# Latent layer: TensorE's transposes of the probabilities are issued behind a step's scores and exponentials, where they were issued in front of them

## The chip, the cores and the metric

The kernel runs on one core of one Trainium2 chip. The metric is the device time of one execution in microseconds (us). The kernel before took 2329.43 us, the median of three runs (2329.16, 2329.43 and 2336.82 us). The profile comes from one more execution, which took 2339.59 us. A core has five engines that matter here: TensorE (PE in the profile, with its weight loads as PEld), VectorE (DVE), ScalarE (ACT), GpSimd (POOL) and SyncE (SP). SyncE does no arithmetic; in this kernel it issues the transfers. Each engine works through its own instructions in the order in which the program issued them, and waits where one of them needs a result or a buffer that isn't there yet.

## The reference

The input is two sequences of 1024 tokens with 128 features. Four attention layers (called a, b, c and d here), each followed by a feed-forward part, are added to it in turn:

```
x = x + attn_a(ln(x));  x = x + ffn(ln(x))     # a: shared keys and values, no mask
x = x + attn_b(ln(x));  x = x + ffn(ln(x))     # b: causal
x = x + attn_c(ln(x));  x = x + moe(ln(x))     # c: causal, "latent"
x = x + attn_d(ln(x));  x = x + moe(ln(x))     # d: causal, with biases
```

All have 16 heads of 64. The change concerns layer c:

```
q      = x @ Wq                       # 16 heads of 64
latent = x @ Wkv_down                 # 32 numbers for each token
k, v   = latent @ Wk_up, latent @ Wv_up
attn   = softmax(where(causal, q @ k.T / 8, min))
out    = (attn @ v) @ Wout
```

The kernel multiplies Wq with Wk_up, and Wv_up with Wout, once at the start. From there on, layer c's keys and values are both the latent itself, and its products contract over, or yield, 32 rows of the array where the other layers have 64.

## The kernel before

**Units and steps.** The work of a layer is cut into units: one sequence and one pair of heads, so 16 units a layer. The queries are 8 tiles of 128. A causal unit has five steps, by their query tiles: [7], [6, 0], [5, 1], [4, 2] and [3]. Tile n sees n + 1 tiles of keys, so the two-tile steps have 8 tiles of keys, and [3] has 4. One loop runs over the steps of all units; its body writes out the order of the work by hand, and the order of each engine's instructions is exactly that of the program (`manual_schedule`).

**What a step does.** Let s be the step that is new. `scores` (L634 for the products, L649 for layer c's masks) multiplies queries with keys on TensorE, into two PSUM buffers `sc`, one for each head h of the pair; in layer c the products of both heads are issued in turns, and the masks of both follow. VectorE finds each row's maximum (L678, `nmax`), and `exponentials` (L689) has ScalarE write exp(score - max) into an SBUF tile `pr`, of which there are two buffers. A step's scores can't start on a head before the exponentials of the step ahead have read that head's `sc`. One step later, `normalize` divides: a reciprocal on VectorE (L697), and four (or two) multiplications on GpSimd (L701). Two steps later (`st` is step s - 2) the probabilities are transposed so that they can be multiplied with the values.

**Two ways to transpose.** The queries are grouped in four blocks of 256 (qb, two tiles each). Blocks 2 and 3 (tiles 4 to 7) of a causal layer are "blocked": VectorE transposes 32 x 32 pieces of `pr` into `slots` (L771), and when both tiles of a block are there, `blocks_moved` has SyncE issue 16 transfers from `slots` to `prT` (L746). Blocks 0 and 1 (tiles 0 to 3) go through TensorE: 128 x 128 transposes into a PSUM tile `pp` (L788), for two tiles of keys at most and both heads, and a copy by ScalarE into `prT` or `prT_four` (L789). Tile 0 takes 2 transposes and 1 copy, tile 1 takes 4 and 1, tile 2 takes 6 and 2, and tile 3 takes 8 and 2. `pp` is one of the uses of a pool of three PSUM buffers, in turn with the projections, the output products and the feed-forward part.

**Where they stand.** Because `st` is two steps back, tile 0 is transposed when [4, 2] is new, tile 1 when [3] is, and tiles 2 and 3 when the next unit's [7] and [6, 0] are; when [5, 1] is new there is only VectorE's part. In the loop body, `transposes(st)` comes first. Then come GpSimd's additions to x (`add_products`, L889), perhaps an early piece of the feed-forward part (`side_part`), then `scores` and `exponentials` of s, then `out_product` (L866 and a copy, L873), a piece of the next unit's projection (L532, L540), pieces of the feed-forward part, and the products with the values for blocks that were completed earlier (`weigh`, L836 and L840 in layer c, and a copy of their sum, L856). Which blocks may be weighed is kept in `late`: a block gets its `ready` step when both of its tiles are transposed, at once for blocks 0 and 1 and two steps on for the blocked ones, whose transfers take time. The products with the values of block 3 so stand in the [7] and [6, 0] of the next unit, those of blocks 0 and 1 in its [5, 1], and those of block 2 in its [4, 2].

Of the kernel before, what the change touches and what calls it, by code (L numbers as in the profile page):

```python
# [27 lines left out]
TPA = AB // P  # L28
# [8 lines left out]
def kernel(ctx: ExitStack, tc: tile.TileContext, a: dict, out: bass.AP):  # L37
# [223 lines left out]
    def moe_group(nm, b, g, last, xT, eng=nc.gpsimd, other=None):  # L261
# [139 lines left out]
    layers = [  # L401
        dict(nm="a", causal=False, kind="shared", ffn=dense_group, fnm="f"),
        dict(nm="b", causal=True, kind="full", ffn=dense_group, fnm="g"),
        dict(nm="c", causal=True, kind="latent", ffn=moe_group, fnm="m"),
        dict(nm="d", causal=True, kind="bias", ffn=moe_group, fnm="n"),
    ]
# [37 lines left out]
    def xT_tile(li, b):  # L444
        return lnp.tile([P, S], F32, tag="xT", name=f"xT_{li}{b}", bufs=2)
# [129 lines left out]
    def tag_of(u):  # L575
        li, b, p = u
        return f"{layers[li]['nm']}{b * NPAIR + p}"
# [20 lines left out]
    def blocked(u, qb):  # L598

        if qb not in BLOCKED[layers[u[0]]["kind"]]:  # L600
            return 0
        nk = keys(u, qb * TPA + TPA - 1)
        return nk if layers[u[0]]["causal"] else nk - 1

    def keys(u, qt):
        return qt + 1 if layers[u[0]]["causal"] else NT
# [99 lines left out]
    def prT_of(u, qb):  # L706


        nk = keys(u, qb * TPA + TPA - 1)
        odd = nk == NT and qb % 2 and not layers[u[0]]["causal"]  # L710
        for part in ("second", "rest") if odd else (HOMES[nk],):
            old, held[part] = held.get(part), (u, qb)
            while old:
                if any(x[:2] == old for x in products):
                    weigh_some(4)
                elif any(x["key"] == old for x in late):
                    release()
                else:
                    break
        if odd:  # L720
            return prT_many[1]
        return {
            8: prT_many[0], 6: prT_many[1][:, : 12 * AB], 4: prT_four, 2: prT_many[1][:, 12 * AB :]
        }[nk]

    def blocks_of(u, qb):

        return slots[:, 1 - qb % 2, : 2 * blocked(u, qb) * AB]  # L730
# [23 lines left out]
                copies.append((o, x))  # L754
        probT[u, qb] = t.rearrange("p (i t h c) -> p t h i c", t=TPA, h=2, i=4)

    def transposes(st):

        u, pr = st["u"], st["pr"]
        for qt in st["qts"]:
            qb, cols = qt // TPA, slice(qt % TPA * P, (qt % TPA + 1) * P)
            nk, nb = keys(u, qt), blocked(u, qb)
            for h in range(2 if nb else 0):
                n = min(nk, nb)
                dst = blocks_of(u, qb).rearrange(
                    "p (r t h k q) -> p t h k r q", r=4, t=TPA, h=2, q=32
                )[:, qt % TPA, h, :n]
                src = pr[:, h, st["at"][qt] : st["at"][qt] + n * P]  # L770
                nc.vector.transpose(  # L771
                    dst,
                    src.rearrange("p (k r q) -> p k r q", r=4, q=32),
                )
                yield
            if nb < nk and nb:
                o = rest_of(u, qb)[:, qt % TPA].unsqueeze(2)
            elif nb < nk:
                if (u, qb) not in probT:
                    probT[u, qb] = prT_of(u, qb).rearrange("p (h k q) -> p h k q", h=2, q=AB)  # L780
                o = probT[u, qb][:, :, :, cols]
            for k0 in range(nb, nk, 2):
                k1 = min(k0 + 2, nk)
                pt = ps_m.tile([P, 2, 2, P], F32, tag="pm", name=f"pp_{tag_of(u)}_{qt}_{k0}")
                for h in range(2):
                    for kt in range(k0, k1):
                        c0 = st["at"][qt] + kt * P
                        nc.tensor.transpose(pt[:, h, kt - k0, :], pr[:, h, c0 : c0 + P], ident)  # L788
                nc.scalar.copy(o[:, :, k0 - nb : k1 - nb], pt[:, :, : k1 - k0, :])  # L789
                yield  # L790
            complete[u, qb] = complete.get((u, qb), 0) + 1
            if nb and complete[u, qb] == TPA:
                blocks_moved(u, qb)

    def rest_of(u, qb):

        held["four"] = u, qb
        return prT_four.rearrange("p (n t h q) -> p n t h q", t=TPA, h=2, q=P)[:, qb]
# [131 lines left out]
    def drain(gen):  # L930
        for _ in gen:
            pass

    def some(queue, n):

        while n >= 1 and queue:
            try:
                next(queue[0])
                n -= 1
            except StopIteration:  # L940
                queue.popleft()
        return n
# [3 lines left out]
    def side_part():  # L946


        while side:
            try:  # L950
                said[0] = next(side[0])
                return
            except StopIteration:
                side.popleft()
        said[0] = None

    side, products, outs, waiting, complete, done = deque(), deque(), deque(), deque(), {}, {}
    adds, postponed, copies = deque(), deque(), deque()
    late = deque()
# [16 lines left out]
    def weigh_some(n):  # L976
# [7 lines left out]
        if any(x[-1] for x in [*products][:2]):  # L984
            while not part[-1]:
                part = products.popleft()
                weigh(*part)

    ctx.enter_context(tc.manual_schedule())
    drain(start_batch(0, 0, xT_tile(0, 0)))  # L990
    drain(project(units[0]))
# [93 lines left out]
    for step, (n, u, qts, i, total) in enumerate([*steps, *[(None, None, None, 0, 1)] * 4]):  # L1085
        new = None
        if n is not None:
            if n != last:
                last = n
                some(coming, 9)  # L1090
                if n + 1 < len(units):
                    nu = units[n + 1]
                    if nu[:2] != u[:2]:
                        if nu[0] == 2 and 2 not in weights:
                            wq = wpool.tile([D, H * DH], F32, tag="wq", name="wq_c")
                            nc.sync.dma_start(out=wq, in_=c_wqk.rearrange("d p h c -> d (p h c)"))
                            weights[2] = {"wq": wq}
                        elif nu[0] not in weights:
                            weights[nu[0]] = load_attn(w_names[nu[0]])
                        while nu[:2] not in xTs:  # L1100
                            side_part()
                    coming.append(project(nu))


                    if layers[nu[0]]["kind"] == "shared":
                        when = [0, 0, 1, 0, 1, 0, 0, 0]
                    elif layers[nu[0]]["kind"] == "latent":
                        when = [1, 0, 1, 0, 0]
                    elif total == NT:
                        when = [0, 1, 1, 0, 1, 1, 1, 1]  # L1110
                    else:
                        when = [1, 1, 2, 0, 2]
            new = step_of(u, qts)


        st = waiting.popleft() if len(waiting) == 2 or not new and waiting else None
        if st:
            if st["u"] not in begun:
                begun.add(st["u"])
                begin(st["u"])  # L1120
            for _ in transposes(st):
                if last_step:
                    normalize(last_step.pop())
            for qb in {qt // TPA for qt in st["qts"]}:
                if complete[st["u"], qb] == TPA:
                    x = next(x for x in late if x["key"] == (st["u"], qb))
                    x["ready"] = step + (2 if blocked(st["u"], qb) else 0)
        if last_step:
            normalize(last_step.pop())
        add_products()  # L1130
        if new and said[0] == "early":
            side_part()
            share -= 1
        if new:
            sc, nmaxs = scores(new)
            for h in range(2):
                exponentials(new, h, sc[h], nmaxs[h])
            last_step.append(new)
            waiting.append(new)
        while copies:  # L1140
            nc.scalar.copy(*copies.popleft())
        while outs:
            out_product(*outs.popleft())

        values = new and i >= (total - 2 if total == NT else total - 1)
        if new and coming and not values:
            some(coming, when[i])
        share = min(share + (1.8 if n is None else SIDE[u[0]]), 3.0)
        while share >= 1 and side:
            side_part()  # L1150
            share -= 1
            if said[0]:
                break


        while late and late[0]["ready"] is not None and late[0]["ready"] <= step:
            release()
        weigh_some(4)
        if values and coming:
            some(coming, when[i])  # L1160
# [68 lines left out]
```

## Time and profile before

| what | value |
|---|---|
| median of three runs | 2329.43 us |
| the profiled execution | 2339.59 us |
| its span, first to last instruction | 2337.9 us |
| mean granted TensorE clock | 0.954 |
| TensorE busy | 2133.6 us, 91% |
| VectorE busy | 1718.8 us, 74% |
| ScalarE busy | 1450.8 us, 62% |
| GpSimd busy | 1282.9 us, 55% |

The page gives the busy time of each engine, the span in 40 slices, the chain of work that ended last, and the costliest groups of instructions. Other views of the same trace answer for a part of the span: sums by stretch, the waits (who waited for whom), a group's instructions, and the instructions in order of time. The ends of matmuls are modelled, so a busy TensorE isn't one at its peak. "PEclk" is the clock that TensorE was granted, as a share of full speed. "<-" ahead of a name tells what ended an idle time; "issue" is idle time that nothing in the profile explains.

### The profile page before, as it was taken

Reading aid. Unit: us, or ns where it says so; the run is one execution under the profiler, and the core shown is the slowest. Engines: PE = TensorE matmul, PEld = TensorE weight load, DVE = VectorE, ACT = ScalarE, POOL = GpSimd, SP = SyncE. Lnnn points to the kernel's source line nnn. Section 1 sums busy time; section 2 is a strip of 40 time slices with the busy share of each in tenths; the row PEclk is TensorE's granted clock in tenths of the full one; section 3 lists DMA queues with packets and bytes.
Section 4 is the critical chain, followed back from the end, with each engine's and each line's share of the span. In section 5 each row is a group of like instructions: output and inputs, shape, how many; then the busy total and the mean of one; then the engine's idle time right before and its main releaser. Section 6 shows DMA issues by size and latency. Waiting matters only on the chain.

```text
span 2337.9 us, 43430 instructions
## 1 busy us (share of the span) xinstructions
PE 2133.6 (91%) x14833; PEld 1246.6 (53%) x14833; DVE 1718.8 (74%) x2695; ACT 1450.8 (62%) x3276; POOL 1282.9 (55%) x1723
## 2 busy tenths in 40 slices
PE   6999999999999999999998888888889999999986
PEld 2454444444445666666654454444456666656653
DVE  6979988999986876678668767766666656766544
ACT  3667676666765666666655566565666557665542
POOL 3767666767765554455545545545554446544441
PEclk8999999999999999999998788799899999999997
DMA  5667676666776666666654455544566456655450
GB/s 133 160 152 167 161 171 151 147 149 161 167 195 151 148 155 161 163 154 154 161 119 118 110 127 132 128 115 103 148 159 146 107 123 158 158 119 142 109 135 9
DMA packets 147195, 328.84 MB, mean 141 GB/s; under 512 B 48800, under 2 KB 59296, under 8 KB 146976
## 3 DMA queue, kind: packets, MB, share of 16 engines
q1 hardware_dynamic: 146976, 326.06, 59.0%
q8 instruction: 120, 1.97, 0.4%
q14 instruction: 99, 0.81, 0.1%
HBM read 10.27 MB, written 2.10 MB: 5 GB/s over the span
## 4 chain that ended last, share of the span: by engine, by line
PE 50%; SPq 16%; DVE 13%; ACT 8%; DMA 7%; issue 4%; POOL 2%; ACTq 0%; DVEq 0%; POOLq 0%
SPq L746 15%; PE av_a L845 6%; PE sc_a L634 6%; DMA prT<-slots 5%; PE av_d L845 5%; DVE slots L771 4%; PE sc_d L634 4%; PE sc_b L634 3%; PE av_b L845 3%; ACT pr_c L689 3%; PE sc_c L634 2%; DVE nmax_a L678 2%; DVE nmax_d L678 2%; ACT pr_b L689 2%; PE pp_d L788 2%
## 5 line engine op out<-in xcount | busy, mean ns | idle before, releaser
L689 ACT ACTIVATE pr_a<-sc_a,nmax_a 128x1024 f32<-128x1024 f32 x256 | 282.9, 1109 | 216.7 <-DVE nmax_a L678 212.8
L701 POOL TENSOR_SCALAR pr_a<-pr_a,rec_a 128x1024 f32<-128x1024 f32 x256 | 283.4, 1118 | 189.7 <-DVE rec_a L697 189.3
L701 POOL TENSOR_SCALAR pr_d<-pr_d,rec_d 128x1024 f32<-128x1024 f32 (+7 forms) x256 | 186.3, 745 | 271.0 <-DVE rec_d L697 270.7
L678 DVE TENSOR_REDUCE nmax_a<-sc_a 128x1 f32<-128x1024 f32 x256 | 298.7, 1205 | 36.1 <-PE sc_a L634 35.6
L701 POOL TENSOR_SCALAR pr_c<-pr_c,rec_c 128x1024 f32<-128x1024 f32 (+7 forms) x256 | 186.9, 747 | 222.5 <-DVE rec_c L697 222.5
L701 POOL TENSOR_SCALAR pr_b<-pr_b,rec_b 128x1024 f32<-128x1024 f32 (+7 forms) x256 | 186.8, 747 | 218.4 <-DVE rec_b L697 217.9
L678 DVE TENSOR_REDUCE nmax_d<-sc_d 128x1 f32<-128x1024 f32 (+7 forms) x256 | 177.2, 748 | 152.3 <-PE sc_d L640 152.3
L689 ACT ACTIVATE pr_c<-sc_c,nmax_c 128x1024 f32<-128x1024 f32 (+7 forms) x256 | 186.3, 738 | 164.4 <-DVE nmax_c L678 137.3
L771 DVE STREAM_TRANSPOSE slots<-pr_a 128x896 f32<-128x896 f32 x256 | 278.9, 1093 | 2.3 <-DMA prT<-slots 1.3
L689 ACT ACTIVATE pr_b<-sc_b,nmax_b 128x1024 f32<-128x1024 f32 (+7 forms) x256 | 186.3, 738 | 147.0 <-DVE nmax_b L678 120.4
L634 PE MATMUL sc_a<-k_a,q_a 64*128 64x512 f32 x512 | 266.7, 635 | 11.1 <-ACT pr_a L689 10.8
L689 ACT ACTIVATE pr_d<-sc_d,nmax_d 128x1024 f32<-128x1024 f32 (+7 forms) x256 | 186.4, 738 | 135.0 <-DVE nmax_d L678 131.6
L634 PE MATMUL sc_a<-k_a,qx_a 64*128 64x512 f32 x512 | 264.0, 637 | 4.1 <-DMA qx_a<-q_a 4.0
L678 DVE TENSOR_REDUCE nmax_c<-sc_c 128x1 f32<-128x1024 f32 (+7 forms) x256 | 176.8, 747 | 95.1 <-PE sc_c L649 94.8
L678 DVE TENSOR_REDUCE nmax_b<-sc_b 128x1 f32<-128x1024 f32 (+7 forms) x256 | 176.7, 746 | 88.5 <-PE sc_b L640 88.4
L845 PE MATMUL av_a<-prT,v_a 128*64 128x256 f32 x1792 | 223.8, 389 | 19.3 <-DMA prT<-slots 18.4
L845 PEld LDWEIGHTS av_a<-prT,v_a 128*64 128x64 f32 x1792 | 122.8, 137 | 134.6 <-issue 77.9
L634 PE MATMUL sc_b<-k_b,q_b 64*128 64x512 f32 (+3 forms) x416 | 159.1, 495 | 1.4 <-ACT pr_b L689 1.4
L634 PE MATMUL sc_d<-k_d,q_d 64*128 64x512 f32 (+3 forms) x416 | 159.7, 496 | 0.3 <-ACT pr_d L689 0.3
L634 PE MATMUL sc_b<-kx_b,qx_b 64*128 64x512 f32 (+3 forms) x416 | 153.6, 488 | 0.8 <-ACT pr_b L689 0.6
L634 PE MATMUL sc_d<-kx_d,qx_d 64*128 64x512 f32 (+3 forms) x416 | 154.0, 490 | 0.2
L771 DVE STREAM_TRANSPOSE slots<-pr_b 128x1024 f32<-128x1024 f32 (+3 forms) x128 | 130.5, 1024 | 9.3 <-DMA prT<-slots 8.7
(407 smaller groups left out, 4779.6 us busy)
## 6 DMA issues: line engine op xcount, KB each, us to landing
prT<-slots SPq DMA_DIRECT2D x768, 128.0 KB, 2.3
prT<-slots SPq DMA_DIRECT2D x832, 112.0 KB, 2.2
prT<-slots SPq DMA_DIRECT2D x768, 96.0 KB, 2.1
qx_a<-q_a SPq DMA_DIRECT2D x32, 256.0 KB, 3.6
qx_b<-q_b SPq DMA_DIRECT2D x32, 256.0 KB, 3.6
kx_b<-k_b SPq DMA_DIRECT2D x32, 256.0 KB, 3.4
qx_d<-q_d SPq DMA_DIRECT2D x32, 256.0 KB, 3.6
kx_d<-k_d SPq DMA_DIRECT2D x32, 256.0 KB, 3.5
```

The lines of the kernel that those rows point to most:

```text
L634: yield nc.tensor.matmul(sc[h][:, at[qt] + k0 : at[qt] + k1], lhsT=q[r, qt * P : (qt + 1) * P], rhs=kk[r, k0:k1], start=True, stop=not dia ...
L678: nc.vector.tensor_reduce(out=nmax[:, n : n + 1], in_=sc[h][:, c], axis=AX.X, op=ALU.max, negate=True)
L689: nc.scalar.activation(st["pr"][:, h, c], sc[:, c], AF.Exp, bias=nmax[:, n : n + 1], accum_out=tot[:, h, n : n + 1],)
L701: nc.gpsimd.tensor_scalar(out=pr[:, h, c], in0=pr[:, h, c], scalar1=rec[:, h, n : n + 1], scalar2=1.0, op0=ALU.mult, op1=ALU.mult,)
L746: nc.sync.dma_start(out=o, in_=x)
L771: nc.vector.transpose(dst, src.rearrange("p (k r q) -> p k r q", r=4, q=32),)
L788: nc.tensor.transpose(pt[:, h, kt - k0, :], pr[:, h, c0 : c0 + P], ident)
L845: nc.tensor.matmul(shaped(av[ROWS[h], n], t0), lhsT=vs[u][:, kt, h, :], rhs=moving(h, kt, t0), start=(kt == 0), stop=(kt == nkt - 1),)
```

## The change

`transposes` takes a second argument, which of the two kinds of tiles it is to treat: blocked (True) or not (False). When the tile that is due belongs to a unit of layer c, and there is a new step, only the blocked kind is issued at the old place. The other kind, TensorE's transposes and ScalarE's copies of them, is issued after the new step's scores, maxima and exponentials, ahead of `out_product`. The bookkeeping that sets `ready` becomes a function, `note_complete`, and is called after both kinds are done; it sets the same step numbers. All other layers, and the steps after the last unit, keep the old order. No instruction is added, removed or changed in size.

```
-    def transposes(st):
+    def transposes(st, kinds):
         u, pr = st["u"], st["pr"]
         for qt in st["qts"]:
+            if bool(blocked(u, qt // TPA)) not in kinds:
+                continue
             qb, cols = qt // TPA, slice(qt % TPA * P, (qt % TPA + 1) * P)
...
+    def note_complete(st):
+        u = st["u"]
+        for qb in {qt // TPA for qt in st["qts"]}:
+            if complete[u, qb] == TPA:
+                x = next(x for x in late if x["key"] == (u, qb))
+                x["ready"] = step + (2 if blocked(u, qb) else 0)
...
-            for _ in transposes(st):
+            behind = new and layers[st["u"][0]]["kind"] == "latent"
+            for _ in transposes(st, [True] if behind else [True, False]):
                 if last_step:
                     normalize(last_step.pop())
-            for qb in {qt // TPA for qt in st["qts"]}:
-                if complete[st["u"], qb] == TPA:
-                    x = next(x for x in late if x["key"] == (st["u"], qb))
-                    x["ready"] = step + (2 if blocked(st["u"], qb) else 0)
+            if not behind:
+                note_complete(st)
         if last_step:
             normalize(last_step.pop())
         add_products()
...
         while copies:
             nc.scalar.copy(*copies.popleft())
+        if st and behind:
+            drain(transposes(st, [False]))
+            note_complete(st)
         while outs:
             out_product(*outs.popleft())
```

## The prediction

> **What bounds the kernel now.** I read the sums by stretch first, since only layer c is touched. Layers b and c are these rows (stretch, length, busy us of PE, PEld, DVE, ACT, POOL with counts, granted clock, DMA share, GB/s):
>
> ```profile
> 692.00:1192.00 500.00, 480.51 (x3668) 321.36 (x3667) 358.80 (x601) 324.21 (x808) 261.02 (x395) 0.99 0.65 154
> 1192.00:1697.00 505.00, 426.63 (x3306) 236.32 (x3304) 361.23 (x613) 302.69 (x774) 270.61 (x411) 0.86 0.53 124
> ```
>
> Layer c takes 505 us for 16 units, 31.5 us each. TensorE is idle for 78 us of it and has a mean clock of 0.86, which is half clock for 140 us: no engine is full, so waits bound it. Next the waits of that stretch (waiter, releaser: us, times, longest):
>
> ```profile
> ACT pr_c L689 <- DVE nmax_c L678: 137.3, 59, 5.5
> ...
> PE pp_c L788 <- POOL pr_c L701: 18.1, 21, 2.7
> ```
>
> ScalarE waits in nearly every step for the maximum, so for the scores. TensorE waits 21 times at the transposes to be moved. In order of time, TensorE from [3]'s masks to the next unit's [7]:
>
> ```profile
> 1434.30 0.28 PE L649 MATMUL sc_c<-over_all,ident_b 128*128 128x128 bf16 x2
> 1434.42 0.70 PE L866 MATMUL po_c<-wo_c,attnT_c 128*128 128x128 f32 x4
> 1435.33 0.44 PE L788 MATMUL pp_c<-ident,pr_c 128*128 128x128 f32 x2 [0.21 <-POOL pr_c L701]
> 1436.67 1.12 PE L788 MATMUL pp_c<-ident,pr_c 128*128 128x128 f32 x4 [0.90 <-POOL pr_c L701]
> 1437.71 2.09 PE L634 MATMUL sc_c<-latT_c,q_c 32*128 32x512 f32 x8
> 1439.74 0.38 PE L649 MATMUL sc_c<-over_all,ident_b 128*128 128x128 bf16 x2
> 1439.92 1.10 PE L532 MATMUL pq_c<-xT,wq_c 128*128 128x512 f32 x2
> 1442.00 1.07 PE L840 MATMUL av_c<-prT,lat_c 128*32 128x256 f32 x16 [0.97 <-DMA prT<-slots]
> ```
>
> The last exponential of [3] ended at 1436.7, but [7]'s scores start at 1437.71, behind six transposes that stood waiting for GpSimd's division. One unit earlier, at [6, 0] and [5, 1]:
>
> ```profile
> 1415.04 1.09 PE L788 MATMUL pp_c<-ident,pr_c 128*128 128x128 f32 x8
> 1416.06 1.36 PE L634 MATMUL sc_c<-latT,q_c 32*128 32x384 f32 x12
> ...
> 1420.58 1.13 PE L634 MATMUL sc_c<-latT,q_c 32*128 32x256 f32 x4 [1.84 <-ACT pr_c L689]
> ```
>
> Last, the chain of waits from 1433 to 1443. Ahead of these rows it is SyncE's issues, 0.59 and 0.04 us each:
>
> ```profile
> 1437.69 1.86 SPq L746
> ...
> 1439.60 2.31 DMA prT<-slots
> ```
>
> So the products with the values at 1442.00 waited for block 3's sixteen transfers. VectorE had filled `slots` at 1428.83 and the last landed at 1441.91: 13.1 us (11.8 to 13.5 in the other units). That is a second chain beside scores, maxima and exponentials, and the change doesn't touch it.
>
> **The change part by part.** Work stays the same; 20 transposes and 6 copies a unit move, and no transfer does. I went through the instruction times of all 16 units. SyncE's issues hang on VectorE's transposes, which keep their order, as do GpSimd's division and additions.
>
> *Scores go first.* At [4, 2] two transposes take 0.37 us between their start and the scores'; TensorE is late there in 12 of 16 units. At [3] four take 0.6, but in 11 units the second head's scores wait for exponentials anyway. At [7] six, with the wait for GpSimd, hold the scores up by 0.4 to 1.5 us in 11 units, more in one and by nothing in three, where VectorE comes later still. At [6, 0] eight take 1.02.
>
> *What of it is kept.* In 8 of 15 unit changes the products with block 3's values start 1.6 us or less after the landing (0.1 in four). What is gained at [4, 2], [3] and [7] is lost there; only [6, 0]'s eight transposes, which stand behind these products, come off the path: 8 x 1.02 = 8.1. The other 7 have 3.9 to 7.1 us to spare and keep 3.7 at [7] (less the 0.6 that [3]'s four now take behind [3]'s scores), 7 x 0.37 = 2.6 at [4, 2], 1.0 at [3], and at [6, 0] 1.2 (1.02 each, less the 0.85 that [7]'s six now take behind [7]'s scores). Sum 16.6.
>
> *What the transposes delay now.* They stand ahead of the output product, the projection and the products with values. Behind [6, 0], 1.09 us falls into TensorE's idle time ahead of [5, 1], 27.1 us over the 16 units; in two units there is too little, which costs 2.0. If that cover were gone everywhere it would be 16 x 1.09 = 17. Net gain 14.6.
>
> *A new wait.* `pr` has two buffers: exponentials of s overwrite what the transposes of s - 2 read, so they now wait for transposes that stand behind their own scores. From the last mask's end to the first exponential there are 0.77 us at [3], 1.30 at [7], 1.33 at [4, 2] and [6, 0]. The transposes need about 0.85, 1.05, 0.6 and 1.3 with the 0.2 us of hand-over (two ended at 1345.80 and their copy began at 1345.99). So 16 x 0.08 = 1.3 at [3] at full clock. At half clock (eight took 1.86, four 1.17) it is 0.5 at [3], 0.7 at [6, 0], 0.3 at [7]; half clock is now seen at these places in 1, 2 and 9 units, which makes 4. Behind the waiting exponentials on ScalarE stand the copies of `pp`, of sums and of projections, and the next scores wait for them. I take 5.3, between 1.3 and 1.3 + 24 (half clock everywhere).
>
> *Copies of `pp`* run after the exponentials, in the 1.7 to 3.9 us in which ScalarE waits for the next maximum (137.3 us in all): 0.4 to 1.2 us each step, at no cost. If that cover were gone, they cost 46 us, their busy time in this stretch (L789).
>
> *The clock.* These rows are TensorE's granted windows (the sixth column group is the clock):
>
> ```profile
> 1433.14:1436.55 3.41, 1.90 (x12) 1.14 (x12) 2.91 (x5) 2.90 (x8) 2.63 (x4) 1.00 0.92 207
> 1436.55:1439.97 3.42, 3.30 (x15) 1.47 (x15) 0.96 (x3) 1.37 (x5) 3.32 (x5) 0.50 0.64 141
> ```
>
> After 1.90 us of work in 3.41 the next window ran at half. Over the stage, windows below half busy are nearly always followed by half clock, those above 0.7 hardly ever. The change shifts idle time out of the waits ahead of [7] and [5, 1], but lengthens the one for the transfers, behind which [6, 0]'s scores would then run at half. Bounds: half clock gone altogether gives 140 x 0.28 (TensorE's share of this stretch's chain) x 0.5 = 20 gained; half clock at [6, 0] in the 8 units bound by transfers costs 8 x (0.77 for the scores + 0.7 for the wait above) = 12. Between, I take the share by which idle time falls, 14.6 of 78, of those 20: 4 gained.
>
> A rule speaks against this credit. The Trainium skill, "TensorE: Matmul & The Clock Gate", Part 4, says transposes don't count as TensorE being busy in the way that matmuls do. By it, transposes moved into the idle time ahead of [5, 1] leave the half clock where it is, and the sum would be 9.3 instead of 13.3. The row differs: this window kept full clock behind it (1354.56 onwards at 1.00), and half its work was transposes (first all work, then L788 alone):
>
> ```profile
> 1351.15:1354.56 3.41, 2.52 (x24) 1.72 (x23) 2.89 (x5) 2.75 (x9) 2.93 (x5) 1.00 0.66 149
> ...
> 1351.15:1354.56 3.41, 1.26 (x8) 0.81 (x9) 1.00 0.66 149
> ```
>
> *Sum.* 14.6 - 5.3 + 4 = 13.3 us less. The profiled execution, 2339.59 us (span 2337.9 and 1.7 around it), would take 2326.3. It lies 10.2 above the median of the runs, so from the median: 2329.43 - 13.3 = 2316.1. A measurement tells about 0.5% (11.6 us) from no change.
>
> **Rivals.**
>
> *The clock opens.* If the idle time ahead of [7] and [5, 1] was what kept TensorE at half, it runs at full speed: 14.6 + 20 - 1.3 = 33 less, 2296. For it: those two places precede most half-clock windows. Against: the wait for the transfers grows.
>
> *Given back.* Block 3's transfers hold 8 units where they are, and TensorE, idle ahead of 1442.00 for up to 2 us, does [6, 0] at half clock: 13.3 less the 12 above, 2328. For it: 0.1 us between landing and products in four units. Against: there the landing also came behind a slow [7].
>
> *Slower: exponentials wait for transposes.* The place is L689 behind L788 through `pr`. It decides from 14.6 / 48 = 0.3 us a step at [7], [6, 0] and [3], and makes the kernel measurably slower from 26.2 / 48 = 0.55. At half clock everywhere it is 24, and if at [7] and [6, 0] the transposes also wait for a copy of `pp` (0.59 us) to free a PSUM buffer, 32 x 0.59 = 19 more: 24 + 19 + 1.3 - 14.6 = 30 at most, about 19 in the middle: 2348. For it: 0.77 us at [3] leave nothing over. Against: at full clock the others fit.
>
> **How the numbers follow.** Chances: forecast 0.5, the clock opens 0.17, given back 0.2, slower 0.13. The forecast's own range is 2304 to 2326 (half the net gain, or twice it). The range for 8 in 10 reaches from 2291, below the open clock's time, to 2342, where less than 1 in 10 lies above. Faster by over 0.5% (under 2317.8): 0.17, three fifths of the forecast's half, and a little of the third, 0.49. Slower: most of the last, 0.12. Within: 0.39.
>
> **What would show it.** In the profile after: the wait of `pp` for GpSimd (18.1 us) all but gone; [7]'s scores at most 0.3 us behind [3]'s last exponential; the wait of `av_c` for transfers up from the 3.2 us it shows; layer c's clock above 0.86; stage 1192 to 1697 shorter by 13 us and the others alike. ScalarE waiting at L689 for TensorE's L788 would show the new wait. The forecast fails if the stage's clock falls, or if TensorE rather than the transfers turns out late in the 8 units.

## The result, and the profile after

The changed kernel takes 2337.95 us (median of 12 runs, 2335.09 to 2345.33), the kernel before in the same rounds 2330.76 us (12 runs). The ratio is 1.0033, with a 95% interval from 1.0022 to 1.0044: some 7 us slower, where 13 us faster was forecast. The profiled execution took 2341.42 us, its span 2339.7 us.

The sums by stretch of the kernel after, over the stretches that the prediction showed (stretch, length, busy us of PE, PEld, DVE, ACT, POOL with counts, granted clock, DMA share, GB/s):

```profile
692.00:1192.00 500.00, 480.04 (x3661) 320.82 (x3660) 357.83 (x599) 323.83 (x805) 260.88 (x393) 0.99 0.64 153
1192.00:1697.00 505.00, 411.38 (x3246) 227.06 (x3246) 355.58 (x606) 297.00 (x759) 267.43 (x405) 0.90 0.51 121
```

Layer b is as it was. In layer c the clock has risen from 0.86 to 0.90, and yet less is done in the same 505 us: TensorE is idle for 94 us (505 less 411) and not for 78. From its first scores to its last exponential the layer takes 511.0 us, 6.2 more than in the profile before.

The waits of the same stretch of the kernel after (waiter, releaser: us, times, longest):

```profile
ACT pr_c L689 <- DVE nmax_c L678: 131.9, 60, 6.4
...
DVE hid_m L366 <- PE uu_m L361: 17.8, 10, 3.8
...
PE uu_m L361 <- DVE sg_m L357: 13.7, 8, 2.2
...
PE av_c L842 <- DMA prT<-slots: 9.4, 5, 2.2
...
ACT pr_c L689 <- PE pp_c L790: 6.3, 2, 3.8
...
PE pq_c L532 <- DVE sg_m L357: 4.6, 2, 2.3
...
PE pp_c L790 <- POOL pr_c L701: 0.9, 1, 0.9
```

The wait of the transposes for GpSimd has gone from 18.1 us to 0.9. Two waits have grown. The products with the values wait 9.4 us for transfers, as the forecast said. The other is new in size: `uu_m`, the up product of the experts in layer c's feed-forward part, waits eight times for VectorE's `sg_m`. In the profile before it waited twice, and `cb_m`, the coefficients' product behind it, five times:

```profile
PE cb_m L372 <- DVE sg_m L357: 4.8, 5, 1.3
PE uu_m L361 <- DVE sg_m L357: 4.4, 2, 2.2
```

So some of this wait has only moved, from `cb_m` to `uu_m`. Over all products, TensorE waited 12.2 us for `sg_m` before (with 1.7 at `gg_m` and 1.3 at `po_m`) and 18.3 after.

The loss has a place. I cut layer c into its 16 units, each from the end of one [3]'s exponentials to the end of the next. The experts' loop (L352 to L376) runs as side work in units 10 to 13 (counted from 0), with two, three, one and four of its ten turns before, and the second of two routers (L282) in unit 12. Units 11, 12 and 13 took 38.3, 29.6 and 40.6 us before, and 44.2, 33.0 and 49.4 after: 18.1 us more. The other thirteen, unit 10 among them, took 396.3 before and 384.4 after: 11.9 us less. Here are the sums over units 11 to 13, of the kernel before,

```profile
1528.10:1636.60 108.50, 91.45 (x717) 52.23 (x716) 72.21 (x120) 62.79 (x157) 54.87 (x74) 0.94 0.44 103
```

and of the kernel after:

```profile
1520.60:1647.20 126.60, 101.57 (x717) 54.52 (x715) 72.75 (x120) 63.47 (x157) 54.53 (x73) 0.88 0.38 88
```

The number of matmuls is the same, 717. Idle time of TensorE rises from 17.0 us (108.50 - 91.45) to 25.0. The clock falls from 0.94 to 0.88, so half clock lasts 30 us and not 13 (twice the missing share of the clock, times the length), and half of the 17.4 added is lost: 8.7 us. Those two make 16.7 of the 18.1. Two of the eight waits of `uu_m`, 3.0 us, stand in unit 10, which became 0.6 us shorter all the same; it had waited 1.8 us at `cb_m` before.

One such place in order of time, unit 11 at [6, 0], in the kernel after:

```profile
1532.50 0.59 PE L352 MATMUL gg_m<-xT,m_gate 128*128 128x512 f32 x1
...
1534.10 0.40 PE L649 MATMUL sc_c<-over_all,ident_b 128*128 128x128 bf16 x4
...
1534.33 1.04 PE L790 MATMUL pp_c<-ident,pr_c 128*128 128x128 f32 x8
1534.42 2.49 DVE L678 TENSOR_REDUCE nmax_c<-sc_c 128x1 f32<-128x896 f32 x4 [2.90 <-PE sc_c L649]
...
1536.82 0.68 DVE L357 SCALAR_TENSOR_TENSOR sg_m<-sg_m,gg_m 128x512 f32<-128x512 f32 x1
...
1537.56 2.08 PE L361 MATMUL uu_m<-xT,m_up 128*128 128x512 f32 x2 [2.18 <-DVE sg_m L357]
...
1538.47 1.08 ACT L791 COPY prT_four<-pp_c 128x512 f32<-128x512 f32 x2
1539.56 0.10 PEld L372 LDWEIGHTS <-sel 24*128 24x128 bf16 x1 [1.50 <-issue]
1539.57 0.60 PE L372 MATMUL cb_m<-cfT_m,sel 24*128 24x512 bf16 x1
```

and in the kernel before:

```profile
1539.03 0.40 PE L649 MATMUL sc_c<-over_all,ident_b 128*128 128x128 bf16 x4
...
1539.26 1.08 PE L361 MATMUL uu_m<-xT,m_up 128*128 128x512 f32 x2
...
1540.27 0.38 PE L372 MATMUL cb_m<-cfT_m,sel 24*128 24x512 bf16 x1
```

The transposes' `pp`, the gate product `gg`, the up product `uu` and the coefficients' product `cb` all take turns in one pool of three PSUM buffers. Before, `pp` was copied out at once, and `uu` followed the masks without a gap. After, at 1535.4 all three buffers are full: two `pp`, which ScalarE copies only behind the step's exponentials (1538.47), and `gg`, which VectorE reads only behind the step's maxima (1536.82). TensorE stands for 2.18 us. What follows then runs at half speed (the granted clock is 0.50 from 1537.56 to 1540.20): `uu` takes 2.08 us and not 1.08, `cb` 0.60 and not 0.38. The next scores stand behind them in TensorE's queue.

The theory to be tested is this one: **the buffers are held**. The rivals: the half clock has merely moved to other places; the exponentials wait for the transposes through `pr` (the prediction's slower rival); and the transposes' own place in TensorE's queue, between the scores and the experts' products, does it.

### The profile page after: what moved, and what is told of

Same layout as the page of the kernel before. It is cut to its first block, busy times and chain, and to the rows that moved or that the text cites. A ratio compares the mean times of both kernels' runs of the same rounds, so it can differ in the third digit from the quotient of the medians.

```text
span 2339.7 us, 43436 instructions
## 1 busy us (share of the span) xinstructions
PE 2118.5 (91%) x14833; PEld 1238.6 (53%) x14833; DVE 1717.7 (73%) x2695; ACT 1451.1 (62%) x3276; POOL 1286.9 (55%) x1723
## 4 chain that ended last, share of the span: by engine, by line
PE 52%; SPq 15%; DVE 14%; ACT 9%; DMA 6%; issue 4%; POOL 1%; DVEq 0%; ACTq 0%; POOLq 0%
SPq L746 14%; PE sc_a L634 6%; PE av_a L847 6%; PE av_d L847 5%; DMA prT<-slots 4%; DVE slots L773 4%; PE sc_d L634 4%; ACT pr_c L689 4%; PE av_b L847 3%; PE sc_b L634 3%; PE sc_c L634 3%; DVE nmax_d L678 2%; DVE nmax_a L678 2%; DVE nmax_c L678 2%; PE pp_d L790 2%
## 5 line engine op out<-in xcount | busy, mean ns | idle before, releaser
L847 PE MATMUL av_a<-prT,v_a 128*64 128x256 f32 x1792 | 223.0, 388 | 18.3 <-DMA prT<-slots 17.6
```

Of the source, the lines that this page charges most:

```text
L847: nc.tensor.matmul(shaped(av[ROWS[h], n], t0), lhsT=vs[u][:, kt, h, :], rhs=moving(h, kt, t0), start=(kt == 0), stop=(kt == nkt - 1),)
```

## The experiments

All edits are against the kernel after, unless said otherwise. "11-13" and "other 13" are sums of unit lengths of layer c from one profile each, in us; the ratio is that of the timed runs to the kernel before in the same rounds, with its 95% interval.

| kernel | transposes | copies | median us | ratio | 11-13 | other 13 |
|---|---|---|---|---|---|---|
| before | in front | at once | | 1 | 108.5 | 396.3 |
| before, profiled again | in front | at once | | | 108.4 | 391.2 |
| after | behind | late | 2337.95 | 1.0033 (1.0022 to 1.0044) | 126.6 | 384.4 |
| e6 | behind, not in the experts' loop | as after | 2325.11 | 0.9975 (0.9961 to 0.9989) | 109.6 | 384.3 |
| e7 | behind in the experts' loop alone | as after | 2342.36 | 1.0047 (1.0034 to 1.0061) | 118.7 | 393.4 |
| e3 | behind for tiles 0, 1 | as after | 2338.04 | 1.0025 (1.0012 to 1.0038) | 113.1 | 395.3 |
| e4 | behind for tiles 2, 3 | as after | 2333.49 | 1.0018 (1.0003 to 1.0033) | 117.5 | 383.9 |
| e12 (and e2) | behind | ahead of exponentials | 2317.98 | 0.9928 (0.9903 to 0.9952) | 99.9 | 382.3 |
| e15 | behind | ahead in the experts' loop alone | 2324.43 | 0.9957 (0.9941 to 0.9974) | 105.8 | 384.7 |
| e16 | in front | late | 2391.98 | 1.0247 (1.0228 to 1.0265) | 138.9 | 417.5 |
| e10 | behind, gate read early | late | 2330.38 | 0.9986 (0.9972 to 1.0001) | 112.4 | 380.1 |
| e11 | in front, gate read early | at once | 2325.18 | 0.9965 (0.9953 to 0.9978) | 100.6 | 388.4 |
| e13 | behind, gate read early | ahead of exponentials | 2313.22 | 0.9904 (0.9878 to 0.9929) | 94.9 | 375.9 |

### How far one profile can be trusted

The kernel before, profiled once more.

> The kernel before once more, for how far two profiles of one kernel differ by unit of the latent layer. Both theories: the sum over units 11 to 13 within 3 us of 108.5 us, that over the other thirteen within 5 us of 396.3 us; if the spread is wider, the 18 us are no finding.

Measured: 2335.7 us; units 11 to 13 in 108.4 us, the others in 391.2 us. Its sums over units 11 to 13 are nearly those of the first profile:

```profile
1524.30:1632.70 108.40, 91.46 (x717) 52.11 (x716) 72.22 (x120) 62.83 (x158) 54.94 (x74) 0.94 0.45 103
```

So the 18.1 us in these units are a finding. The other thirteen differ by 5.1 us between two profiles of one kernel (the first unit alone by 4.8); the gain there is 7 to 12 us, not 11.9.

### Where the loss sits: e6, e7

```
+        experts[0] = True
         hid = []
         for c in range(NE // 2 + 1):
...
+        experts[0] = False
         apply_coefficients()
...
-            behind = new and layers[st["u"][0]]["kind"] == "latent"
+            behind = new and layers[st["u"][0]]["kind"] == "latent" and not experts[0]
```

`experts[0]` is true while the experts' loop is under way. In e6 the transposes of those steps go back in front of the scores.

> The transposes stand behind the scores in every step but those in which the matmuls of the experts' loop are being issued (units 11 to 13 of the latent layer); there they stand in front, as before. Theory of the held buffers (the probabilities' transposes keep two of the three shared PSUM buffers until ScalarE has finished the step's exponentials, and the experts' gate and up products, which use the same three, wait): units 11 to 13 cost what they cost before the change, the other thirteen keep their 11.9 us, so about 12 us faster than the kernel before, 2318 to 2324 us, ratio 0.995. Theory of the shifted half clock (the loss is where the gate's windows happen to fall, not tied to the experts): the thirteen units and the three move anew, 0 to 7 us slower than before, ratio 1.000 to 1.003. Theory of the wait on the probabilities' own buffers: the loss sits at the step with the least slack in any unit, so the loss stays, ratio 1.002 to 1.003.

e7 has `and experts[0]` in its place.

> The reverse: the transposes stand behind the scores only in the steps in which the experts' loop issues its matmuls, and in front of them in all others. Theory of the held buffers: the loss of units 11 to 13 alone, about 18 us slower than before, ratio 1.0075 (2346 to 2350 us), with VectorE's waits for the up product and TensorE's waits for VectorE's sigmoid product as in the kernel after. Theory of the shifted half clock: within 4 us of before, ratio 0.998 to 1.002. Theory of the wait on the probabilities' own buffers: a fifth of the units have it, so 1 to 2 us slower, ratio 1.0005.

Measured: e6 is 0.25% faster than before, e7 0.47% slower. In e6 units 11 to 13 are back at 109.6 us, and the other thirteen keep the whole gain of the kernel after (384.3 against 384.4). In e7 the thirteen are as before, and the three lose 10 us. The waits of e7 in units 11 to 13 are those of the kernel after (its lines are one or two further down):

```profile
DVE hid_m L367 <- PE uu_m L362: 14.1, 8, 3.3
PE uu_m L362 <- DVE sg_m L358: 10.7, 6, 2.2
PE pq_c L534 <- DVE sg_m L358: 4.6, 2, 2.3
```

So the loss is tied to the steps in which the experts' products are issued, and a shift of half clock alone or a wait through `pr` in every unit is ruled out as its main part. The times moved by half to two thirds of what the theory expected. One reason is in unit 12, which has the router and only one turn of the loop: it takes 33.2 us in e6 as in the kernel after (33.0), and 29.6 in e7 as before. What it waits for is in e6's waits of units 11 to 13, the same in the kernel after:

```profile
PE pr_m L282 <- ACT prT_four L793: 2.6, 1, 2.6
```

The router's product waits for the copy of a transpose by name.

### One buffer or two: e3, e4

```
-            behind = new and layers[st["u"][0]]["kind"] == "latent"
+            behind = new and layers[st["u"][0]]["kind"] == "latent" and min(st["qts"]) < 2
```

> Only the steps that follow tiles 0 and 1 keep their transposes behind the scores (one PSUM buffer of transposes each, at the steps of tiles 4 and 2 and of tile 3); tiles 2 and 3, with two buffers each, are transposed in front, as before. Theory of the held buffers: one buffer held leaves the experts' products two, so no loss in units 11 to 13, and the small gains of these two steps stay: 0 to 4 us faster than before, ratio 0.998 to 1.000. Theory of the wait on the probabilities' own buffers: tile 3's step has the least slack there (0.77 us), so most of the loss is here, 4 to 7 us slower, ratio 1.002 to 1.003. Theory of the shifted half clock: anything within 7 us to either side.

e4 has `min(st["qts"]) >= 2`.

> The reverse: only tiles 2 and 3, with two PSUM buffers of transposes each, are transposed behind the scores (at the steps of tile 7 and of tiles 6 and 0 of the next unit); tiles 0 and 1 in front. Theory of the held buffers: the whole loss of units 11 to 13 is here (18 us), and so is most of the gain of the others (about 9 of 12 us), so 6 to 10 us slower than before, ratio 1.003 to 1.004. Theory of the wait on the probabilities' own buffers: no loss, 8 to 12 us faster, ratio 0.995 to 0.997. Theory of the shifted half clock: anything within 7 us to either side.

Measured: e3 is 0.25% slower and e4 0.18%. Of e4 the expectation was right in place and too large in size: the thirteen units hold the whole gain (383.9 us), but the three lose 9.0 us where 18 were expected, and the ratio is 1.0018 where it was to be 1.003 to 1.004. Of e3 it was wrong. One buffer held is enough to lose 4.6 us in units 11 to 13, with five waits of the up product:

```profile
PE uu_m L361 <- DVE sg_m L357: 8.4, 5, 2.2
```

And its thirteen units show no gain: 395.3 us lies between the two profiles of before, whose difference of 5.1 us could hide a gain of 3. By time alone e3 speaks for the rival of `pr`; the copies' experiments below, in which the transposes stand at [3] as here, settle that.

### The copies alone: e2, e12, e15, e16

e2 leaves the transposes behind the scores, and puts their copies ahead of the exponentials.

```
             sc, nmaxs = scores(new)
+            if st and behind:
+                drain(transposes(st, [False]))
+                note_complete(st)
             for h in range(2):
                 exponentials(new, h, sc[h], nmaxs[h])
...
-        if st and behind:
-            drain(transposes(st, [False]))
-            note_complete(st)
```

The order on TensorE is that of the kernel after; on ScalarE six copies a unit have moved forward.

> The transposes stay behind the scores, and their copies out of PSUM go ahead of the step's exponentials on ScalarE, so that their buffers are free some 2 us earlier; the exponentials of two of five steps start up to 1 us later, up to 32 us over the layer. Theory that the experts' products wait for the buffers that the transposes hold: TensorE's waits at the up product (13.7 us in the kernel after) are gone, and units 11 to 13 fall below 120 us. Theory that the up product waits for the gate product's own buffer, which comes round as its own because two transposes were allocated in between, and which VectorE reads only behind the maxima: the waits stay, 8 of about 2 us, and units 11 to 13 stay at 120 us or more.

> The kernel with the copies ahead of the exponentials once more, timed in rounds. Theory of the held buffers: its one run (2317.7 us) stands, ratio to the kernel before 0.992 to 0.995, units 11 to 13 at 99 to 102 us. Rival, that the one run was a low one: ratio 0.997 or more.

Measured: e2 took 2317.71 us in one run, e12, which is the same kernel, 2317.98 us as the median of its rounds, 0.72% faster than before. Units 11 to 13 take 99.7 and 99.9 us. TensorE's waits at the up product for VectorE fall from 13.7 us to 3.6. The same place as above, unit 11 at [6, 0], in e12:

```profile
1528.34 1.04 PE L790 MATMUL pp_c<-ident,pr_c 128*128 128x128 f32 x8
1528.43 2.48 DVE L678 TENSOR_REDUCE nmax_c<-sc_c 128x1 f32<-128x896 f32 x4 [3.13 <-PE sc_c L649]
...
1528.98 1.07 ACT L791 COPY prT_four<-pp_c 128x512 f32<-128x512 f32 x2 [1.19 <-PE pp_c L790]
...
1529.62 1.13 PE L361 MATMUL uu_m<-xT,m_up 128*128 128x512 f32 x2 [0.24 <-ACT prT_four L791]
...
1530.83 0.68 DVE L357 SCALAR_TENSOR_TENSOR sg_m<-sg_m,gg_m 128x512 f32<-128x512 f32 x1
```

The up product now starts 0.24 us late, at full clock, on the copy of the transposes and 1.2 us ahead of VectorE's read of the gate product. The theory that only the gate's own buffer matters falls. The sums of units 11 to 13 in e12 show where the 26.7 us against the kernel after come from: 11.6 us idle and not 25.0, at a clock of 0.98 and not 0.88.

```profile
1518.70:1618.60 99.90, 88.27 (x715) 50.11 (x714) 72.48 (x120) 62.57 (x157) 55.15 (x74) 0.98 0.48 112
```

Between the ratios of the kernel after and of e12 lie 0.0105, which is 24.5 us at 2333 us (18 to 31 by the two intervals): the late copies cost that, and units 11 to 13 alone account for it. The exponentials, which now stand behind the copies, cost nothing that shows: the other thirteen units take 382.3 us. They were hardly delayed, since ScalarE would have waited for the maxima meanwhile: from the last mask's end to the first exponential most units have 0.96 us at [3] where the kernel after has 0.79 or 0.80, and 1.44 at [6, 0] where that mostly has 1.33.

e15, with the same `experts[0]` as e6, puts the copies ahead only while the experts' loop runs.

```
+            ahead = experts[0]
...
+            if st and behind and ahead:
+                drain(transposes(st, [False]))
+                note_complete(st)
...
-        if st and behind:
+        if st and behind and not ahead:
```

> The copies go ahead of the exponentials only in the steps in which the experts' loop issues its matmuls; in all other steps they stay behind the exponentials, as in the kernel after. Theory of the held buffers: units 11 to 13 as with all copies ahead (99 to 102 us), the other thirteen as in the kernel after (384 us): ratio 0.992 to 0.995. Rival, that the gain of the early copies comes from earlier transposed probabilities in every unit: the quiet units show it, and this kernel is 5 us or more slower than with all copies ahead, ratio 0.995 to 0.998.

Measured: 0.43% faster than before, units 11 to 13 in 105.8 us, the others in 384.7. It misses e12's 99.9 by 5.9 us, of which 5.6 are in unit 12 (33.3 against 27.6), where the router's product waits 2.6 us as in e6. By time alone the rival holds: the ratio of 0.9957 lies in its range and outside that of the theory, and the median is 6.4 us above e12's. But the rival put that loss in the quiet units, and the other thirteen are within 2.4 us of e12's, less than two profiles of one kernel differ by. So the held buffers account for most of the gap, through the router, which the expectation had left out.

e16 starts from the kernel before. Nothing moves on TensorE; only the copies go behind the exponentials.

```
-                nc.scalar.copy(o[:, :, k0 - nb : k1 - nb], pt[:, :, : k1 - k0, :])
+                o_x = o[:, :, k0 - nb : k1 - nb], pt[:, :, : k1 - k0, :]
+                if new and layers[u[0]]["kind"] == "latent" and not nb:
+                    copies.append(o_x)
+                else:
+                    nc.scalar.copy(*o_x)
```

> The fourth cell: the transposes stand in front of the scores, as in the kernel before, and only their copies out of PSUM go behind the step's exponentials. Theory of the held buffers: the buffers are held longer than in any other kernel, while no instruction of TensorE has moved; units 11 to 13 take 118 to 130 us (108.4 and 108.5 in two profiles of the kernel before), with TensorE's products of the feed-forward part waiting for ScalarE's copies, the other thirteen units take 391 to 400 us as before, ratio 1.004 to 1.010. Rival, that the loss comes from the transposes' place in TensorE's queue, between the scores and the experts' products: nothing has moved there, so units 11 to 13 as before and ratio 0.999 to 1.001.

Measured: 2.47% slower, 59 us. Units 11 to 13 take 138.9 us, with the waits of the kernel after, longer on average:

```profile
PE uu_m L361 <- DVE sg_m L357: 13.9, 7, 3.1
...
PE pq_c L532 <- DVE sg_m L357: 6.0, 2, 3.0
PE pr_m L282 <- ACT prT_four L1145: 3.2, 1, 3.2
```

The rival of the transposes' place falls: none of TensorE's instructions has moved, and the same products wait. But the loss is larger than expected, and the other thirteen units, which were to stay as before, lose 21 to 26 us too. An instance at [6, 0] of unit 7, which has no such products:

```profile
1425.87 1.07 PE L844 MATMUL av_c<-prT,lat_c 128*32 128x256 f32 x16 [0.69 <-DMA prT<-slots]
...
1427.76 0.85 ACT L1145 COPY prT_four<-pp_c 128x512 f32<-128x512 f32 x2
...
1428.44 1.06 PE L788 MATMUL pp_c<-ident,pr_c 128*128 128x128 f32 x8 [1.50 <-issue]
1429.44 1.14 PE L634 MATMUL sc_c<-latT,q_c 32*128 32x384 f32 x8
```

The step's transposes stand 1.50 us, with the scores behind them. The profile names no releaser here, but ScalarE's first copy of the transposes of the step ahead ended at 1428.34, 0.1 us ahead of their start. All waits of this kind in layer c are like it:

```profile
PE pp_c L788 <- issue: 23.5, 13, 3.8
```

Each of the thirteen ends 0.1 us after a copy of transposes has ended, so these transposes too wait for a buffer that a late copy holds. The profile of the kernel before has no such wait at the transposes. One of these waits, 1.9 us, stands in unit 12; the other twelve, 21.6 us, stand outside units 11 to 13, where 21 to 26 us are lost.

The four cells of order and copies, by ratio: in front with copies at once 1, behind with late copies 1.0033, in front with late copies 1.0247, behind with early copies 0.9928. The new order is worth 0.7% where the copies are early and 2.1% where they are late. The change made both steps at once.

### The third buffer: e10, e11, e13

The third buffer is the gate product's, which VectorE reads behind the maxima. Here VectorE's read is issued with the gate product, ahead of them.

```
             nc.scalar.activation(sg, gg, AF.Tanh, scale=0.5)
-            yield
             nc.vector.scalar_tensor_tensor(
                 out=sg, in0=sg, scalar=1.0, in1=gg, op0=ALU.add, op1=ALU.mult
             )
+            yield
```

> The kernel after, with VectorE's read of the gate product issued with the gate product, ahead of the step's maxima, where it stood behind them. Theory of the gate product's own buffer: the waits of the up product for VectorE are gone, units 11 to 13 take 108 to 112 us, and the kernel is 10 to 14 us faster than before, ratio 0.994 to 0.996. Theory of the buffers that the transposes hold: the up product gets the free buffer and the next product needs one that a transpose holds until ScalarE is through its exponentials, so the wait moves to the coefficients' product, about as long (2.6 us); units 11 to 13 take 118 to 126 us, ratio 1.001 to 1.003.

e11 makes the same edit to the kernel before.

> The kernel before (transposes in front of the scores) with the same early read of the gate product, as the counterpart. Both theories: in this order the up product has the first transpose's buffer, long free, so the early read takes only the 4.4 us of waits at the up product and part of the 2.9 us at VectorE: 0 to 6 us faster than before, ratio 0.9975 to 1.000, units 11 to 13 at 103 to 108 us. If it were as much faster as the kernel with the transposes behind and the early read is against the kernel after, the early read would be a gain of its own and no evidence on the buffers.

Measured: e10 is 0.14% faster than before (its interval just includes no change), e11 0.35%. In e10 the waits for VectorE's `sg_m` are gone, but some of them come back as waits for the transposes' copies:

```profile
DVE hid_m L366 <- PE uu_m L361: 6.9, 2, 3.6
PE uu_m L361 <- ACT prT_four L791: 5.3, 2, 2.7
```

With 112.4 us in units 11 to 13 and a ratio of 0.9986, both between the two expectations, both kinds of held buffer count. The early read is a gain of its own, 7.9 us in those units of the kernel before and 14.2 in those of the kernel after; e11's gain was larger than expected. With it, the change still costs the three units 11.8 us (112.4 against 100.6), and the kernel 0.2%.

e13 has both remedies, the copies ahead of the exponentials and the early read.

> Copies ahead of the exponentials, and VectorE's read of the gate product ahead of the maxima. Theory of the held buffers: all three buffers come free early, so the last waits of the up product (3.6 us) go too; 0 to 5 us faster than with the copies ahead alone, ratio to before 0.990 to 0.994, units 11 to 13 at 96 to 100 us. Rival, that the early read is bought with later maxima: units 11 to 13 as with the copies alone or up to 4 us longer, ratio 0.993 to 0.996.

Measured: 2313.22 us, 0.96% faster than before (0.71 to 1.22%), the lowest median here, though its interval overlaps that of e12. Units 11 to 13:

```profile
1512.10:1607.00 94.90, 87.60 (x714) 51.44 (x714) 72.34 (x119) 62.39 (x158) 55.35 (x74) 0.96 0.52 120
```

TensorE is idle for 7.3 us of them, where it was 17.0 before and 25.0 after.

## Why the prediction was wrong

*Scores go first, and what of it is kept.* Right in sum, though not in its parts. Net 14.6 us over the layer would be some 12 in thirteen of sixteen units; with half clock counted, the whole forecast of 13.3 would be 10.8 there. The thirteen units gained 11.9 against one profile of before and 6.8 against the other. The kernel that has the new order without held buffers (e12) has a ratio of 0.9928, where the forecast amounts to 0.9943; but 8.6 us of its gain are in units 11 to 13, where an even share of the forecast would be 2.5, so this nearness is partly luck. Tiles 0 and 1 ([4, 2] and [3]), to which 3.6 us were given, show no gain in e3, and e4 has the whole of it with [7] and [6, 0] alone. [7]'s scores now start when [3]'s exponentials release them: 1431.93 in the rows below, 0.74 us of waiting for ScalarE and no transposes ahead.

```profile
1430.58 0.61 PE L868 MATMUL po_c<-wo_c,attnT_c 128*128 128x128 f32 x4
1431.93 1.80 PE L634 MATMUL sc_c<-latT_c,q_c 32*128 32x512 f32 x8 [0.74 <-ACT pr_c L689]
1433.65 0.29 PE L649 MATMUL sc_c<-over_all,ident_b 128*128 128x128 bf16 x2
1433.78 0.82 PE L790 MATMUL pp_c<-ident,pr_c 128*128 128x128 f32 x6
1434.44 1.02 PE L532 MATMUL pq_c<-xT,wq_c 128*128 128x512 f32 x2
1437.68 1.34 PE L842 MATMUL av_c<-prT,lat_c 128*32 128x256 f32 x16 [2.22 <-DMA prT<-slots]
1438.96 2.09 PE L634 MATMUL sc_c<-latT_c,q_c 32*128 32x384 f32 x12
```

*What the transposes delay now* was priced by their time on TensorE alone, 2.0 us net. Ahead of [5, 1] TensorE's idle time did fall, from 27.1 to 17.7 us. But in units 11 to 13 it is not the transposes' 1 us that delays the feed-forward part's products; it is the buffer behind them.

*A new wait*, priced at 5.3 us (1.3 to 25.3): close to nothing. The exponentials waited twice by name for transposes, and the 6.3 us shown there are those in which the scores and maxima weren't there either. At [3] they start 0.79 or 0.80 us behind the last mask in thirteen units, where it was 0.77 or 0.78. Of the two, one started at the usual distance, and the other (1.79 us where 1.33 is usual) cost 0.5 us. (The parts of the 4 us given to half clock add up to 4.6 as they are printed: 0.5 + 2 x 0.7 + 9 x 0.3.) The slower rival had its sign right and its place wrong; e12, with the same transposes behind the same scores, is faster than before.

*Copies of `pp`* "at no cost" is the step that failed: the copies were put at nothing. I asked whether ScalarE has idle time for them, which it has, and not what the three PSUM buffers do while the copies wait. The copy of a `pp` began 0.2 us after its transposes had ended, and now begins when the exponentials are through: 3.1 us at the place shown above (1535.4 to 1538.47). Measured, between the kernel after and e12, it costs 24.5 us, in the three units in which the feed-forward part wants the same buffers. The 46 us that I named as the price if the cover were gone were the copies' own time on ScalarE, which is not what was paid. The pool's size stood in the text on the kernel; a buffer of it came up only inside the slower rival, as a wait of the transposes.

*The clock.* A credit of 4 us was given for less half clock. It did go up, 0.86 to 0.90 over the stage, while units 11 to 13 went from 0.94 to 0.88, which alone lost 8.7 us. The layer has 140 us of half clock in the first profile of before, 119 in the second and 102 after. How much the rest brought can't be separated, since two profiles of one kernel differ by 20 us. No run here tells whether transposes count for the clock.

*The other rivals.* The clock did not open: 2296 was never near. The transfers did hold [6, 0] more often (five waits of 9.4 us in all, where it was three of 3.2), as "given back" had it: above, the products with the values wait 2.22 us for them and the scores behind run at half clock, 2.09 us for what takes 1.14 elsewhere. In units 7 to 9 TensorE's idle time at [6, 0] is 6.4 us, and was 2.2 and 0.9 in the two profiles of before. But e12 gains its 0.72% with the same transfers (8.7 us of that wait), so this isn't what decided.

## What to carry to other kernels

When work is moved behind something else, follow not only the engines that it runs on but the buffers that it keeps: a PSUM tile is in use until its copy, and a copy that fits into idle time of its engine can still starve whoever shares the pool. Look for those users in every part of the stage, side work that runs in a few units included, and price the move there and not in a typical unit. If producers move behind a critical step, let the instructions that empty their buffers move only as far as needed.

## What the runs showed that I had not expected

A copy's place alone, six small instructions a unit on an engine with idle time, moved the kernel by 1.05% behind the scores and by 2.47% in front of them, without any other instruction moving. Half clock made the idle time about twice as dear: of the 18.1 us in units 11 to 13, 8.0 are TensorE standing idle, and 8.7 are work in these units at half speed. And the exponentials, which looked like the chain that must not be touched (ScalarE's 137.3 us of waits for the maxima before), can have copies ahead of them with no loss that shows: the copies fit into that wait, and the exponentials of e12 start only 0.1 to 0.2 us later.
